# A four-layer graph network on one core: the transpose of layer 2's input moved from TensorE to VectorE and DRAM, layer 0's scaling from VectorE to ScalarE and GpSimd, and a new written order

## The chip, the core and the metric

The kernel runs on one core of a Trainium2 chip. The core has TensorE (PE in the profile, with its weight loads as PEld), VectorE (DVE), ScalarE (ACT), GpSimd (POOL) and SyncE (SP), which here does nothing but issue DMAs; 16 DMA engines move the data. The metric is the time of one execution on the device in microseconds. Before the change the median of three runs is 553.37 us (552.64 to 554.17).

## The reference

32 graphs of 512 nodes with 128 features, all with the same 0/1 adjacency matrix, pass through four layers. Each layer ends with x = layernorm(x + f(x)). In short:

```python
x = _layernorm(x + _L0_gnn_ref(x, adj, ...))   # attention, bias, leaky_relu(0.3)
x = _layernorm(x + _L1_gnn_ref(x, adj, ...))   # attention, elu
x = _layernorm(x + _L2_gnn_ref(x, adj, ...))   # (A*M) @ (x W0) + (A*(1-M)) @ (x W1) + bias
x = _layernorm(x + _L3_gnn_ref(x, adj, ...))   # ((adj @ x + x) W + bias), rows scaled to length 1
```

Layers 0 and 1 form h = x W, two numbers per node, logits leaky_relu(e_src + e_dst, 0.2) masked by the adjacency, a softmax over a row, and the product with h. In layer 2, A is a softmax over the edges of a row (all edges weigh the same for the given inputs) and M the identity, so that a node's own features go through W0 and its neighbours' through W1.

## The kernel before

**Tiles.** A graph is a tile of 128 partitions by 512 columns: four chunks of 128 nodes, side by side. A product with the adjacency over 512 nodes needs 4 x 4 blocks. Where the features have to stand on the partitions, as the stationary side of a product with a weight matrix, x has to be transposed first, for each graph and for layers 0, 1 and 2.

**Units.** The work is written as small named units, each with the tiles it uses (`unit("tb1", "dt1", "xt1")`). For each graph b:

- `ld` and `lb` load x, plainly (L156) and in runs of 32 numbers (L162); `tr0` transposes blocks of 32 x 32 on VectorE (L166), so that `xt0` has layer 0's input transposed.
- `ph0a/b` (L200) form h and its two extra columns, `ex` (L204) their exponentials, `h` (L210) the scaled h. `rt`, `rw`, `rb` (L235, L239, L243) spread a row of exponentials over all partitions by way of DRAM; `al0r` (L255) forms the attention weights on VectorE.
- `po0a/b` (L217) are the attention products, a half of the nodes each; the sum of the weights comes as an extra column and `rs0a/b` (L221) take its reciprocal. `v0a/b` (L262) scale by it and add the bias b0 on VectorE, two instructions per half; `lr` (L272) is the leaky relu, `add0` (L286, GpSimd) the residual, `bn0`, `ms0`, `le0`, `lx0`, `nm0` (L360 to L378) the statistics and `nrm0` (L383, ScalarE) the normalised x1.
- Layer 1 is the same, with x1 transposed by way of DRAM in graphs 3 to 29: `tr1` (L182, VectorE, 32 x 32 blocks), `tw1` (L186, one DMA to DRAM), `tb1` (L192, four DMAs back). In graphs 0, 1, 2, 30 and 31 it goes through TensorE: `pt1` (L174, four transposes into a PSUM bank) and `xt1` (L178, a copy on ScalarE). Its scaling is done on ScalarE (`v1as/v1bs`, L268), and GpSimd normalises x2 (`nrm1p0` to `p3`, L390).
- Layer 2: `xh2` and `xl2` (L292, L296) split x2 into two parts for a fast product, `py2` (L303) multiplies both with the adjacency without its diagonal, `y2` (L307) copies the result. `pt2` and `xt2` (L174, L178) transpose x2 itself, in all 32 graphs. `po2` (L317, L318) adds y2 W1 and xt2 W0 in one PSUM bank; `o2s` (L397) scales by the reciprocal degree, `xb` and `v2p` (L311, L401, GpSimd) add bias and residual.
- Layer 3: `xh3`, `xl3`, `py3`, `y3`, `po3` (L324), `v3` (L328), squares and their root on ScalarE (L334 to L346), `rr0` to `rr3` (L353), `bn3`, `nrm3p0` to `p3` (L390) and the store `st` (L473).

**Order.** Nothing schedules the program but two tables: `STARTS` has a number for each unit that is run once (loads of weights, the transposed adjacency in `an0` to `an3` with its copies `cva` and corrections `cvd`, the final flag that sends unusual inputs to a general path), and `PLAN` one number per unit and graph. The units are sorted by that number and written out, and each engine takes its own in that order. A number of -1 leaves the unit out for that graph. Some 14 graphs are under way at a time. All DMAs of the graphs are issued by SP, in order, each after the semaphores that it needs.

**Buffers.** Each kind of tile has a fixed stock (`kind(...)`): 33 of "sq" for most 128 x 512 tiles, six PSUM banks "ps", four "dt" in DRAM. A tile is taken at its first use in the written order and given back after its last; the engines wait for whatever used it before.

Of the kernel before, what the change touches and what calls it, by code (L numbers as in the profile page):

```python
# [10 lines left out]
F32 = mybir.dt.float32  # L11
# [3 lines left out]
AF = mybir.ActivationFunctionType  # L15
# [3 lines left out]
P = 128  # L19
# [7 lines left out]
def kernel(  # L27
# [87 lines left out]
    def kind(name, count, names, make):  # L115
        STOCK[name] = (count, make)
        for n in names.split():
            KIND[n] = name
# [19 lines left out]
    kind("dt", 4, "dt1", lambda name: dram.tile([P, N], F32, name=name))  # L138
# [4 lines left out]
    def unit(name, *tiles):  # L143
        def register(fn):
            UNITS[name] = (fn, tiles)
        return register
# [33 lines left out]
    @unit("tr1", "x1", "tr1")  # L180
    def _(b, x1, tr):
        nc.vector.transpose(tr.rearrange("p (f c i) -> p c f i", f=NCH, c=NCH), x1)  # L182
# [5 lines left out]
    @unit("tb1", "dt1", "xt1")  # L188
    def _(b, dt, xt):
        for f in range(4):  # L190
            src = bass.AP(tensor=dt.tensor, offset=dt.offset + f * P, ap=[[N, Q], [Q * N, P // Q], [1, P]])
            nc.sync.dma_start(xt[f * Q : (f + 1) * Q, :].rearrange("p (a n) -> p a n", n=P), src)  # L192

# [63 lines left out]
    for half, s in enumerate("ab"):  # L257
# [6 lines left out]

        @unit(f"v1{s}s", f"po1{s}", f"rs1{s}", "o1")
        def _(b, p, rs, o, half=half):
            for c in range(2):
                nc.scalar.activation(chunks(o)[:, 2 * half + c, :], twos(p)[:, c, :F], AF.Copy, scale=rs[:, c : c + 1])  # L268

# [367 lines left out]
    def _(b, p):  # L637
# [3 lines left out]
        "ja": 1, "warm": 2, "awt0": 6, "awc0": 8, "rest": 9, "e2": 10, "awq0": 12, "e0": 13, "am2": 14, "en2": 15,  # L641
        "e1": 16, "aws0": 17, "am0": 18, "e3": 19, "en0": 20, "am1": 24, "eh": 25, "wb": 28, "am3": 29, "m3": 30,
        "m0": 31, "m2": 32, "m1": 33, "en1": 39, "mp": 45, "en3": 46, "an1": 51, "cva1": 54, "dga": 55, "cvd1": 56,
        "deg": 66, "an3": 71, "cva3": 75, "awt1": 80, "cvd3": 81, "awc1": 103, "awq1": 112, "aws1": 116, "an0": 168,
        "cva0": 173, "cvd0": 180, "an2": 270, "cva2": 278, "cvd2": 284, "lpp": 290, "lpd": 357, "de": 525, "dv": 543,
        "out_d": 2946, "out_p": 3099, "out_c": 3104,
    }
    PLAN = {
        "ld": [0, 3, 4, 5, 27, 93, 122, 192, 255, 338, 426, 510, 576, 688, 778, 851, 943, 1020, 1111, 1205, 1308, 1389,
            1469, 1561, 1650, 1741, 1845, 1937, 2020, 2121, 2232, 2281],  # L650
        "pt0": [7, 41, 38, 43, -1, -1, -1, -1, -1, -1, -1, -1, -1, -1, -1, -1, -1, -1, -1, -1, -1, -1, -1, -1, -1, -1,
            -1, -1, -1, -1, -1, -1],
        "xt0": [11, 44, 48, 47, -1, -1, -1, -1, -1, -1, -1, -1, -1, -1, -1, -1, -1, -1, -1, -1, -1, -1, -1, -1, -1, -1,
            -1, -1, -1, -1, -1, -1],
        "ph0a": [21, 57, 76, 77, 125, 132, 166, 264, 331, 420, 496, 608, 640, 747, 831, 941, 1017, 1113, 1200, 1260,
            1416, 1514, 1605, 1701, 1811, 1906, 2017, 2120, 2198, 2312, 2394, 2465],
        "ph0b": [22, 49, 70, 74, 123, 135, 167, 266, 332, 423, 504, 606, 636, 757, 826, 944, 1013, 1118, 1204, 1281,
            1417, 1513, 1603, 1715, 1810, 1908, 2013, 2116, 2200, 2306, 2392, 2528],
        "ex0a": [23, 62, 79, 82, 128, 141, 170, 273, 333, 427, 501, 615, 652, 754, 840, 948, 1024, 1127, 1218, 1280,
            1426, 1523, 1610, 1709, 1820, 1918, 2022, 2127, 2206, 2320, 2404, 2472],  # L660
        "ex0b": [26, 52, 73, 78, 126, 145, 169, 271, 336, 428, 509, 611, 648, 762, 837, 951, 1018, 1123, 1216, 1290,
            1424, 1519, 1609, 1721, 1818, 1915, 2021, 2122, 2205, 2319, 2396, 2536],
        "pc0": [36, 63, 83, 90, 130, 148, 175, 277, 341, 439, 518, 619, 654, 764, 842, 952, 1030, 1130, 1223, 1297,
            1437, 1525, 1617, 1727, 1828, 1923, 2030, 2139, 2208, 2329, 2407, 2538],
        "pr0": [35, 65, 86, -1, -1, -1, -1, -1, -1, -1, -1, -1, -1, -1, -1, -1, -1, -1, -1, -1, -1, -1, -1, -1, -1, -1,
            -1, -1, -1, -1, 2430, 2545],
        "h0a": [42, 68, 87, 95, 131, 156, 184, 289, 345, 447, 530, 635, 658, 767, 859, 957, 1039, 1139, 1236, 1323,
            1441, 1532, 1624, 1736, 1831, 1942, 2038, 2146, 2221, 2338, 2421, 2543],
        "h0b": [37, 64, 84, 91, 133, 150, 177, 283, 342, 441, 519, 621, 655, 765, 844, 953, 1031, 1131, 1225, 1298,
            1438, 1527, 1618, 1728, 1829, 1930, 2031, 2140, 2209, 2330, 2408, 2539],  # L670
        "al0": [40, 72, 96, -1, -1, -1, -1, -1, -1, -1, -1, -1, -1, -1, -1, -1, -1, -1, -1, -1, -1, -1, -1, -1, -1, -1,
            -1, -1, -1, -1, 2434, 2550],
        "po0a": [53, 88, 100, 144, 207, 228, 305, 347, 425, 508, 624, 703, 775, 860, 976, 1022, 1135, 1226, 1309, 1421,
            1517, 1646, 1735, 1815, 1913, 2037, 2137, 2251, 2350, 2435, 2517, 2573],
        "po0b": [60, 98, 114, 159, 215, 253, 320, 364, 453, 554, 646, 716, 795, 908, 960, 1067, 1120, 1263, 1364, 1504,
            1564, 1668, 1767, 1867, 1953, 2066, 2169, 2266, 2366, 2454, 2548, 2641],
        "rs0a": [58, 102, 115, 155, 217, 238, 316, 361, 456, 524, 641, 719, 804, 875, 981, 1048, 1157, 1240, 1329,
            1456, 1534, 1677, 1751, 1869, 1939, 2051, 2172, 2303, 2363, 2450, 2530, 2586],
        "rs0b": [67, 106, 136, 171, 231, 272, 339, 393, 468, 568, 666, 726, 802, 919, 982, 1085, 1165, 1272, 1380,
            1516, 1584, 1685, 1799, 1896, 1964, 2089, 2185, 2294, 2387, 2477, 2565, 2653],  # L680
        "v0a": [59, 107, 117, 178, 232, 248, 322, 362, 465, 529, 643, 728, 811, 885, 987, 1054, 1167, 1248, 1363, 1518,
            1539, 1681, 1777, 1872, 1965, 2059, 2176, 2307, 2370, 2478, 2534, 2591],
        "v0b": [69, 111, 147, 182, 236, 297, 354, 399, 472, 572, 673, 730, 817, 925, 990, 1094, 1178, 1293, 1390, 1544,
            1586, 1688, 1801, 1902, 1970, 2103, 2189, 2322, 2405, 2481, 2572, 2656],
        "lr": [85, 118, 151, 197, 241, 310, 408, 411, 478, 592, 722, 750, 823, 984, 1047, 1146, 1244, 1304, 1448, 1552,
            1596, 1697, 1807, 1917, 1987, 2109, 2212, 2364, 2417, 2486, 2588, 2659],
        "add0": [92, 121, 158, 204, 247, 329, 414, 418, 484, 607, 734, 755, 830, 996, 1057, 1158, 1254, 1319, 1461,
            1563, 1612, 1708, 1813, 1926, 1996, 2119, 2231, 2369, 2422, 2496, 2592, 2663],
# [621 lines left out]
```

## Time and profile before

| | us |
|---|---|
| median of the runs | 553.37 |
| profiled execution | 553.77 |
| its span | 552.1 |
| PE busy | 530.7 |
| DVE busy | 499.1 |
| ACT busy | 472.1 |
| POOL busy | 405.7 |

The granted clock of TensorE over the span is 0.992. The busy time of a group counts each instruction from its start to its end, and instructions of an engine overlap a little; so the cost of a step on a full engine is better read from its start to the next start. Ends of matmuls are modelled. The groups that the change touches, from the page and the answers on lines: the transposes of L174 (164, 148 of them from "sq" tiles, the others from the loaded x), the copies of L178 (41, mean 606 ns), the scale-and-bias of L262 (128, mean 337 ns), the scaling on ScalarE of L268 (128, mean 376 ns), the VectorE transposes of L182 (27, mean 685 ns), and the DMAs of L186 (27 of 256 KB) and L192 (108 of 64 KB). The DMA queue of SP carries 53.94 MB in 123,792 packets, which took 38.4% of the 16 engines' time over the span.

### The profile page before, as it was taken

How to read it: one execution, taken by the hardware profiler on the slowest of the kernel's cores; microseconds unless marked ns; L12 is line 12 of the kernel's file. 1: busy time of each engine (PE TensorE's matmuls, PEld its weight loads, DVE VectorE, ACT ScalarE, POOL GpSimd, SP SyncE). 2: the span in 40 equal slices, each digit the busy share in tenths (PEclk: the TensorE clock that was granted, in tenths of full speed). 3: DMA queues.
4: the chain of work that ended last, by engine and by line, in shares of the span. 5: the costliest groups of instructions: out<-in, count | busy, mean ns of one | idle time of the engine just before them, and what ended most of it. 6: DMA issues, size and time to landing. Idle time of an engine off the chain costs nothing.

```text
span 552.1 us, 13985 instructions
## 1 busy us (share of the span) xinstructions
PE 530.7 (96%) x4116; PEld 501.5 (91%) x4116; DVE 499.1 (90%) x1913; ACT 472.1 (86%) x1868; POOL 405.7 (73%) x673
## 2 busy tenths in 40 slices
PE   7999999999999999999999999999999999999971
PEld 7899999999999999999999999999999999998850
DVE  2799999999999999999999999999999986787475
ACT  3768678988898789888989898898899899989994
POOL 4223795677948868688698776778688878889973
PEclk9999999999999999999999999999999999999996
DMA  7333344536357454446453544545203211000013
GB/s 211 67 83 92 78 117 111 123 93 174 97 136 173 103 139 87 131 112 161 115 136 97 150 106 128 156 99 121 90 20 117 78 39 40 20 21 2 21 57 100
DMA packets 124449, 55.22 MB, mean 100 GB/s; under 512 B 65744, under 2 KB 113488, under 8 KB 124368
## 3 DMA queue, kind: packets, MB, share of 16 engines
q1 hardware_dynamic: 123792, 53.94, 38.4%
q8 instruction: 34, 0.56, 0.4%
q10 hardware_dynamic: 576, 0.33, 0.3%
q14 instruction: 47, 0.39, 0.2%
HBM read 38.67 MB, written 15.58 MB: 98 GB/s over the span
## 4 chain that ended last, share of the span: by engine, by line
PE 76%; DVE 11%; ACT 8%; POOL 2%; issue 1%; DMA 1%; ACTq 0%; DVEq 0%
PE ps L217 37%; PE ps L303 15%; PE ps L200 9%; DVE al L255 4%; PE ps L317 4%; PE ps L318 4%; PE ps L324 4%; PE ps L174 2%; DVE st L360 2%; ACT sq L334 1%; ACT sq L383 1%; DMA acols<-in_L_gnn_a_dst_dram 1%; ACT sq L307 1%; PE ps L230 1%; ACT sq L397 1%
## 5 line engine op out<-in xcount | busy, mean ns | idle before, releaser
L217 PE MATMUL ps<-hp,al 128*128 128x129 f32 x2048 | 244.7, 275 | 0.7 <-POOL off L579 0.5
L217 PEld LDWEIGHTS ps<-hp,al 128*128 128x128 f32 x2048 | 237.4, 191 | 2.7 <-POOL off L579 0.7
L255 DVE SCALAR_TENSOR_TENSOR al<-rb,exps,mp 128x512 f32<-128x512 f32 x216 | 145.6, 735 | 1.2 <-DMA rb<-rd 1.2
L360 DVE BATCH_NORM_STATS2 st<-sq 128x6 f32<-128x128 f32 x508 | 108.2, 274 | 11.1 <-POOL sq L401 7.7
L390 POOL TENSOR_SCALAR sq<-sq,rn 128x128 f32<-128x128 f32 x252 | 113.0, 465 | 3.5
L383 ACT ACTIVATE sq<-sq,rn 128x128 f32<-128x128 f32 x256 | 106.2, 503 | 5.8 <-POOL rn L378 5.6
L210 ACT ACTIVATE hp<-ps,exps 128x128 f32<-128x128 f32 x256 | 89.6, 431 | 0.3
L296 POOL TENSOR_TENSOR xr<-sq,xr 128x512 fp32r<-128x512 f32 x64 | 83.2, 1304 | 7.3 <-DVE st L360 3.8
L200 PE MATMUL ps<-we,sq 128*128 128x131 f32 x512 | 71.2, 277 | 0.1
L303 PE MATMUL ps<-off,xr 128*128 128x512 f32 x256 | 67.6, 406 | 0.0
L303 PE MATMUL ps<-a3t,xr 128*128 128x512 f32 x256 | 67.3, 404 | 0.2 <-POOL xr L296 0.2
L200 PEld LDWEIGHTS ps<-we,sq 128*128 128x128 f32 x512 | 65.4, 192 | 2.0 <-issue 0.5
L286 POOL TENSOR_TENSOR sq<-sq,x 128x512 f32<-128x512 f32 x32 | 41.8, 1307 | 24.0 <-DVE sq L272 13.4
L378 POOL TENSOR_TENSOR rn<-mv,rn 128x4 f32<-128x4 f32 x127 | 28.4, 229 | 41.6 <-ACT rn L374 25.3
L286 POOL TENSOR_TENSOR sq<-sq,sq 128x512 f32<-128x512 f32 x32 | 43.4, 1356 | 17.8 <-DVE sq L280 12.4
L303 PEld LDWEIGHTS ps<-a3t,xr 128*128 128x128 f32 x256 | 46.3, 189 | 10.1 <-POOL xr L296 0.6
L303 PEld LDWEIGHTS ps<-off,xr 128*128 128x128 f32 x256 | 45.9, 189 | 9.1 <-DVE sq L262 0.2
L317 PE MATMUL ps<-w,sq 128*128 128x128 f32 x256 | 49.5, 275 | 0.0
L318 PE MATMUL ps<-w,sq 128*128 128x128 f32 x256 | 49.5, 275 | 0.0
L362 DVE BATCH_NORM_AGGREGATE mv<-st 128x2 f32<-128x9 f32 x508 | 48.7, 157 | 0.0
L401 POOL TENSOR_TENSOR sq<-sq,sq 128x512 f32<-128x512 f32 x32 | 41.1, 1286 | 9.8 <-ACT sq L397 6.9
L268 ACT ACTIVATE sq<-ps,rs 128x128 f32<-128x128 f32 x128 | 39.7, 376 | 8.4 <-DVE rs L221 8.3
(116 smaller groups left out, 918.4 us busy)
## 6 DMA issues: line engine op xcount, KB each, us to landing
rb<-rd SPq DMA_DIRECT2D x54, 256.0 KB, 3.8
x<-in_x_dram SPq DMA_DIRECT2D x32, 256.0 KB, 4.0
out_dram<-sq SPq DMA_DIRECT2D x31, 256.0 KB, 2.3
sw<-in_x_dram SPq DMA_DIRECT2D x112, 64.0 KB, 3.6
dt<-sq SPq DMA_DIRECT2D x27, 256.0 KB, 2.4
sq<-dt SPq DMA_DIRECT2D x108, 64.0 KB, 2.2
rd<-rt SPq DMA_DIRECT2D x54, 2.0 KB, 1.7
an<-in_adj_dram SPq DMA_DIRECT2D x3, 256.0 KB, 4.9
```

The costliest lines, as they stand in the source:

```text
L200: nc.tensor.matmul(twos(p)[:, c, :FE], xt[:, (2 * half + c) * P : (2 * half + c + 1) * P], ATT[k], start=True, stop=True)
L210: nc.scalar.activation(h[:, 2 * half + c, :F], twos(p)[:, c, :F], AF.Identity, bias=pc if k else 0.0, scale=pc)
L217: nc.tensor.matmul(twos(p)[:, c, : F + 1], al[:, j, rows], h[:, j, :], start=(j == 0), stop=(j == NCH - 1))
L255: nc.vector.scalar_tensor_tensor(al[:, j, :], r, exps[:, 2 * b + k, 2, j : j + 1], mask[:, j, :], op0=ALU.max, op1=ALU.mult)
L286: nc.gpsimd.tensor_add(o, o, xk)
L296: nc.gpsimd.tensor_sub(xl, xk, xh.bitcast(F32))
L303: nc.tensor.matmul(p, part[:, j * P : (j + 1) * P], mat[:, j, :], start=(i + j == 0), stop=(i + j == NCH))
L317: nc.tensor.matmul(p[:, cols], y[:, cols], w21, start=True, stop=False)
L318: nc.tensor.matmul(p[:, cols], xt[:, cols], w20, start=False, stop=True)
L360: nc.vector.bn_stats(st[:, c, :6], o[:, c * P : (c + 1) * P])
L383: nc.scalar.activation(xo[:, c * P : (c + 1) * P], o[:, c * P : (c + 1) * P], AF.Identity, bias=rn[:, 1, c : c + 1], scale=rn[:, 0, c : c ...
L390: nc.gpsimd.tensor_scalar(xo[:, c * P : (c + 1) * P], o[:, c * P : (c + 1) * P], rn[:, 0, c : c + 1], rn[:, 1, c : c + 1], op0=ALU.mult, o ...
```

## The change

Three things are changed.

1. In graphs 2 to 30, layer 2's input x2 is transposed as layer 1's is: `tr2` on VectorE in blocks of 32 x 32, `tw2` to DRAM and `tb2` back. The rearrangement is split otherwise than for layer 1: `tw1` writes rows of 2 KB with one DMA and `tb1` reads with four; `tw2` writes with four DMAs, in 512 runs of 128 bytes each, so that `tb2` reads whole rows of 2 KB with one. `pt2` and `xt2` remain in graphs 0, 1 and 31. Layer 1's `tr1`, `tw1`, `tb1` are also used in graphs 2 and 30, where `pt1` and `xt1` go. The stock of DRAM tiles grows from four to six.
2. In graphs 3 to 29, layer 0's scaling by the reciprocal sum is done on ScalarE (`v0as`, `v0bs`: two instructions per half, as `v1as`), and its bias is added after both halves by GpSimd in one instruction over 128 x 512 (`b0p`). In graphs 0, 1, 2, 30 and 31 `v0a/b` remain.
3. Both tables of the order are new.

```diff
-    kind("dt", 4, "dt1", lambda name: dram.tile([P, N], F32, name=name))
+    kind("dt", 6, "dt1 dt2", lambda name: dram.tile([P, N], F32, name=name))
...
-    @unit("tr1", "x1", "tr1")
-    def _(b, x1, tr):
-        nc.vector.transpose(tr.rearrange("p (f c i) -> p c f i", f=NCH, c=NCH), x1)
+    for k in (1, 2):
+
+        @unit(f"tr{k}", f"x{k}", f"tr{k}")
+        def _(b, xk, tr):
+            nc.vector.transpose(tr.rearrange("p (f c i) -> p c f i", f=NCH, c=NCH), xk)
...
+    @unit("tw2", "tr2", "dt2")
+    def _(b, tr, dt):
+        for a in range(NCH):
+            dst = bass.AP(tensor=dt.tensor, offset=dt.offset + a * Q, ap=[[NCH * N, Q], [P, NCH * NCH], [1, Q]])
+            nc.sync.dma_start(dst, tr[a * Q : (a + 1) * Q, :].rearrange("p (g i) -> p g i", i=Q))
+
+    @unit("tb2", "dt2", "xt2")
+    def _(b, dt, xt):
+        nc.sync.dma_start(xt, bass.AP(tensor=dt.tensor, offset=dt.offset, ap=[[N, NCH], [NCH * N, Q], [1, N]]))
...
+        @unit(f"v0{s}s", f"po0{s}", f"rs0{s}", "o0")
+        def _(b, p, rs, o, half=half):
+            for c in range(2):
+                nc.scalar.activation(chunks(o)[:, 2 * half + c, :], twos(p)[:, c, :F], AF.Copy, scale=rs[:, c : c + 1])
...
+    @unit("b0p", "o0")
+    def _(b, o):
+        nc.gpsimd.tensor_tensor(chunks(o), chunks(o), bc(b0_b), op=ALU.add)
```

Of the order, the units run once (the per-graph table changes throughout; the total number of written units goes from 3259 to 3317):

```diff
     STARTS = {
-        "ja": 1, "warm": 2, "awt0": 6, "awc0": 8, "rest": 9, "e2": 10, "awq0": 12, "e0": 13, "am2": 14, "en2": 15,
...
-        "deg": 66, "an3": 71, "cva3": 75, "awt1": 80, "cvd3": 81, "awc1": 103, "awq1": 112, "aws1": 116, "an0": 168,
-        "cva0": 173, "cvd0": 180, "an2": 270, "cva2": 278, "cvd2": 284, "lpp": 290, "lpd": 357, "de": 525, "dv": 543,
-        "out_d": 2946, "out_p": 3099, "out_c": 3104,
...
+        "en0": 29, "mp": 30, "m0": 32, "m3": 33, "en1": 37, "en3": 43, "awt1": 54, "an2": 56, "awc1": 58, "an3": 59,
+        "dga": 60, "awq1": 61, "an0": 62, "aws1": 63, "an1": 64, "cva3": 67, "deg": 68, "cva0": 70, "cvd3": 73,
+        "cva1": 74, "cvd0": 75, "cva2": 78, "cvd1": 80, "cvd2": 86, "lpp": 266, "lpd": 316, "dv": 434, "de": 1002,
+        "out_d": 3020, "out_p": 3156, "out_c": 3177,
     }
```

The numbers count places in the written order, not microseconds.

## The prediction

> **What bounds the kernel now.** I read the page's busy times first, then the chain that ended last, the busy times by stretch, the single instructions in order of time for the cost of a step, and the DMA issues and SP's waits. The page, busy time and the chain's shares by engine:
>
> ```profile
> PE 530.7 (96%) x4116; PEld 501.5 (91%) x4116; DVE 499.1 (90%) x1913; ACT 472.1 (86%) x1868; POOL 405.7 (73%) x673
> ...
> PE 76%; DVE 11%; ACT 8%; POOL 2%; issue 1%; DMA 1%; ACTq 0%; DVEq 0%
> ```
>
> Busy time by stretch (from:to, length, then PE, PE's weight loads, DVE, ACT, POOL with counts; granted clock, DMA share, GB/s):
>
> ```profile
> 175.00:225.00 50.00, 50.00 (x416) 48.53 (x414) 49.82 (x192) 42.77 (x165) 37.10 (x59) 1.00 0.52 123
> 325.00:375.00 50.00, 50.00 (x398) 47.82 (x397) 49.81 (x182) 44.08 (x176) 38.59 (x64) 1.00 0.51 131
> 500.00:520.00 20.00, 19.90 (x135) 17.95 (x134) 13.08 (x71) 19.47 (x82) 20.00 (x27) 1.00 0.05 15
> 540.00:552.10 12.10, 0.48 (x2) 0.29 (x2) 6.33 (x32) 5.99 (x33) 3.29 (x9) 0.63 0.30 92
> ```
>
> In the middle PE is full at full clock and DVE nearly so; ACT has 12 to 14% free, POOL 23 to 26%. The chain in order of time is made of PE pieces alone from 125 to 480 us, and of mixed pieces after:
>
> ```profile
> 473.17 3.57 PE ps L217 x32
> 478.52 1.87 PE ps L303 x8
> 480.87 2.73 DVE al L255 x4
> ```
>
> So PE sets the pace. From start to next start, a half of the attention product (16 matmuls) takes 1.785 us, a half of h 0.447, the two aggregations 1.95 each, po2 1.78, po3 0.89, four transposes 0.44. One graph: 4 x 1.785 + 4 x 0.447 + 2 x 1.95 + 1.78 + 0.89 + 0.44 = 15.9 us; all steps sum to 527. I laid the start of each PE step in the trace beside the sum of the PE work written before it: PE is 6 us late at its first ph0, 10 late at 33 us of work, and stays 8 to 11 late up to py3 of graph 29. It loses time only at both ends: 10 us at the start, about 4 before the last py3 (starts at 535.4), and 16.7 from there to the end.
>
> **The change, part by part.** Step costs from instructions in order of time (start, duration, engine, line):
>
> ```profile
> 259.90 0.60 PE L174 MATMUL ps<-ident,sq 128*128 128x128 f32 x4
> 260.34 1.84 PE L217 MATMUL ps<-hp,al 128*128 128x129 f32 x15
> 260.95 0.65 ACT L178 COPY sq<-ps 128x512 f32<-128x512 f32 x1
> 261.43 0.70 ACT L268 ACTIVATE sq<-ps,rs 128x128 f32<-128x128 f32 x2
> ...
> 207.44 0.60 DVE L262 SCALAR_TENSOR_TENSOR sq<-ps,rs,b_b 128x128 f32<-128x128 f32 x2
> 207.96 0.86 DVE L360 BATCH_NORM_STATS2 st<-sq 128x6 f32<-128x128 f32 x4
> ...
> 200.71 0.70 DVE L182 STREAM_TRANSPOSE sq<-sq 128x512 f32<-128x512 f32 x1
> 201.33 2.67 DVE L255 SCALAR_TENSOR_TENSOR al<-rb,exps,mp 128x512 f32<-128x512 f32 x4
> ...
> 212.04 1.12 ACT L268 ACTIVATE sq<-ps,rs 128x128 f32<-128x128 f32 x4
> 213.12 0.18 ACT L204 ACTIVATE exps<-ps 128x6 f32<-128x6 f32 x1
> ```
>
> Start to next start: a set of four PE transposes 0.44 us, its copy on ACT 0.48, a scale-and-bias pair on DVE 0.52, a DVE transpose 0.62, four scalings on ACT 1.08.
>
> PE: pt2 goes in 29 graphs and pt1 in 2 more (graphs 2 and 30): 31 x 0.44 = -13.6 us. Each set also held one of the six PSUM banks; I count no gain for that, as PE doesn't wait for a bank in the middle.
>
> DVE: 27 graphs lose two pairs, 27 x 1.04 = -28.1; 31 transposes come, 31 x 0.62 = +19.2; net -8.9. Per graph PE drops by 0.44 and DVE by 0.42: should the 99% on DVE be the bound and not PE, the gain is nearly the same.
>
> ACT: +27 x 1.08 = +29.2, less 31 copies, -14.9; net +14.3, or 0.6 per graph. From 44.1 of 50 us it does 14.0 us per 15.9; it would do 14.6 per 15.5. I cost it at nothing because PE's work covers it; with the cover gone it costs up to 0.6 per graph, 16 us.
>
> POOL: b0p is a 128x512 two-input add, as L311 (1.28 us each on the page): +27 x 1.28 = +34.6; 12.3 per graph becomes 13.6. Hidden as well; the cover is 1.9 us per graph. The Trainium skill speaks against it ("SBUF — State Buffer", Who interferes with whom): a DVE instruction with two SBUF inputs and a GpSimd instruction that reads SBUF exclude each other for a whole instruction. Such DVE steps are lr (L272, mean 721 ns) and elu (L280, 771), beside 681 for L328, one input of which is in PSUM: 0.04 to 0.09 us each with POOL at 77%. By the row, POOL at 88% adds about 1 us in all; by the rule, each b0p holding up one DVE step for its 1.28 us, 35. I take the row.
>
> The waits that come with it: b0p waits on POOL for v0bs, with norm pieces and residual adds of other graphs behind it; lr then waits on DVE for b0p, with the al of other graphs behind it, for which PE's product waits. The new order leaves a median of 4 us of PE work between b0p and lr, at least 1.8.
>
> SP and DMA: per graph four tw2 issues like the 128-byte loads of sw and one tb2 like dt, and in two graphs a tw1 and four tb1. Tiles by name, duration min/median/max in ns; the page's DMA issues with us to landing; SP's waits:
>
> ```profile
> L162 SPq DMA_DIRECT2D sw<-in_x_dram x112: 422/488/2226, 13.2 to 383.1; - x112
> ...
> sw<-in_x_dram SPq DMA_DIRECT2D x112, 64.0 KB, 3.6
> dt<-sq SPq DMA_DIRECT2D x27, 256.0 KB, 2.4
> ...
> SPq L243 <- DMA rd<-rt: 33.0, 25, 3.0
> SPq L192 <- DMA dt<-sq: 11.7, 11, 2.6
> ```
>
> 4 x 0.49 + 0.35 = 2.3 us of SP per graph. By the medians of their lines SP issues per graph ld 0.44, sw 4 x 0.49, rd 2 x 0.48, rb 2 x 0.36, dt 0.35, tb1 4 x 0.43 and the store 0.40, 6.5 us now, and waits for landings (33.0 + 11.7) / 27 = 1.7; it would be 10.5 of 15.5 plus the new wait of tb2 for tw2. Behind tb2 on SP stand rb (DVE's al waits for it) and tb1 (PE's ph1 waits for it).
>
> DMA engines: the trace's packets of 128 bytes took a mean 14 ns (58,208 of them), those of 512 bytes 28, of 2 KB 111. tw2 is 2048 of the first, tb2 128 of the last: (28.7 + 14.2) / 16 = 2.7 us per graph on a share of 0.51, so 0.69. Here a rule of the Trainium skill weighs more: "DMA: Bandwidth & Descriptors", Specifications, wants 512 bytes for line rate and says that below this an engine reads, modifies and writes. The only short writes to DRAM in this trace are rd's; the 96 such packets after 390 us, where no sw load runs, took 12 ns each, less than the reads. By the row tw2 is 1.8 us of all engines; by the rule, a 512-byte read and a write for each run, 2 x 28 = 56 ns, 7.2 us, and the share 1.0 (8.1 + 7.2 + 0.9 = 16.2 us per 15.5). I take the row, since it is a write of this very kind.
>
> Order: the early steps an0 to an3 with their copies and corrections, of which two sets came at places 168 to 284 in the old order, now all lie within the first graphs: 0.9 us on PE, 2 on ACT, 1.8 on POOL, at a time when ACT is busy 18.5 of 25 us (25 to 50): 0 to 1 us, I take 0.
>
> The end: when the old order reaches po1a of graph 31 (485.6 us, 477.2 of PE work done), 49.8 us of PE and 53.1 of ACT work are left, 45.6 and 46.1 of it before the last py3, which took 49.8: ACT's work plus 3.7. The new order has 474.4 of PE work before that step, 39.1 of PE and 43.3 of ACT left, 34.9 and 37.3 of it before py3: its last graphs lie further forward. So po1a at 474.4 + 8.4 = 482.8, py3 at 482.8 + 37.3 + 3.7 = 523.8, and the end 16.7 later: **span 540.5**, 11.6 less than 552.1. Of the 13.6 taken from PE about 2 are lost because ACT, with more to do, sets the end. The profiled execution is 553.77 for a span of 552.10, the runs' median 0.4 below it: 540.5 + 1.67 - 0.4 = 541.8, **542 us**.
>
> **Rivals.** First, *SP held by tw2* (slower). One queue issues in order, and tb2 must see tw2 landed. SP has 15.5 - 10.5 = 5.0 us per graph for that wait; with more than 5.4 the kernel is slower than now (15.9 per graph). A landing takes 2.4 (dt) to 3.6 us (sw), and the new order puts 4.5 us or more of PE work between tw2 and tb2, 6.3 in the median, filled with other issues; against it, sw issues of up to 2.2 us show that bursts of short runs hold SP, and the new order has four tw2 and a sw load within 10 us of PE work. At a 6 us wait: 16.5 per graph, 29 x 0.6 = +17, 570 us. The rule's price for a write would lead here too.
>
> Second, *PE waits for xt1*: tb1 to ph1 has a median of 5.0 us of PE work between (8.4 before), at least 3.6, and a tb1 takes 1.3 to its last issue and 2.2 to land. With landings 1 to 2 us later nearly each graph would show it. PE's loss is the greatest lateness, not the sum, while SP keeps its rate: 5 to 9 us, so 547 to 551. Third, *nothing gained*: ACT or the chain through b0p takes the pace and 13 us come back as waits: 553.
>
> **How the numbers follow.** Forecast 0.70 (537 to 547), second rival 0.10, third 0.06, first 0.14. About 0.3% (1.7 us) can be told from no change. Faster 0.80, same 0.06, slower 0.14. The low end, 537, is all 13.6 and 3 us less of drain; the range reaches to 553 to take in the second and third rival and leave out 0.2.
>
> **What would show it.** Right: L174 down to about 40 transposes, PE's sum down by 14 and still 50 of 50 in the middle, ACT at 47 and POOL at 43 to 44 of 50, DMA share near 0.7, SP's wait for the landing of tw2 below 60 us in all. Wrong: idle time of PE ahead of L200 or L217 ended by xt or al, a DMA share at 0.9 or more, rb or tb1 landing 2 us later than now, or sw and tw2 issues held for microseconds.

## The result and the profile after

The changed kernel takes **600.92 us** in the median (597.98 to 602.2) beside 553.0 for the kernel before: a ratio of 1.086 (95% interval 1.081 to 1.090). The forecast was 542, faster. The profiled execution took 600.56 us for a span of 598.9. New line numbers of the units that matter: `tr1`/`tr2` L184, `tw1` L188, `tb1` L194, `tw2` L200, `tb2` L204, `ph` L212, `po` L229, `rw` L251, `rb` L255, `al` L267, `v0as`/`v0bs` L280, `b0p` L289, `lr` L293, `po2` L338 and L339.

The page after, busy times and the chain's shares by engine and by line:

```profile
PE 538.0 (90%) x3992; PEld 503.0 (84%) x3992; DVE 495.6 (83%) x1836; ACT 484.5 (81%) x1945; POOL 442.5 (74%) x700
...
PE 34%; DVE 22%; DMA 20%; ACT 11%; SPq 6%; POOL 4%; issue 3%; DVEq 0%; ACTq 0%; POOLq 0%
PE ps L229 17%; DMA sq<-dt 9%; DVE al L267 9%; PE ps L324 6%; PE ps L212 5%; DMA rb<-rd 4%; DVE st L381 4%; DMA rd<-rt 4%; ACT sq L404 2%; PE ps L339 2%; PE ps L338 2%; PE ps L345 2%; DVE sq L184 2%; SPq L200 2%; ACT hp L222 1%
```

The counts are as the change says: 124 matmuls fewer on PE (31 x 4), 27 more additions on POOL. But no engine is full any more. The chain, 76% PE and 1% DMA before, is now 34% PE and 20% DMA, with 6% in SP's issues.

Busy time by stretch of the kernel after (columns as before):

```profile
175.00:225.00 50.00, 41.08 (x301) 38.10 (x299) 40.84 (x150) 39.15 (x150) 35.23 (x56) 0.97 0.57 134
325.00:375.00 50.00, 46.02 (x344) 43.51 (x344) 38.86 (x143) 43.61 (x178) 39.28 (x63) 0.97 0.58 137
575.00:599.00 24.00, 9.19 (x40) 6.67 (x40) 14.98 (x77) 14.91 (x82) 12.24 (x28) 0.67 0.27 80
```

From 175 to 225 us PE does 301 matmuls where it did 416 before, and the share of the DMA engines is 0.57, less than the 0.69 forecast: the engines as a whole are not full. All of the loss is in the middle. The last `py3` of the kernel starts at 581.8 and the end comes 17.1 us later; before, it was 535.4 and 16.7.

What was waited for on the compute engines (us in total, times, longest), after:

```profile
DVE al L267 <- DMA rb<-rd: 21.8, 12, 5.5
POOL sq L422 <- ACT sq L418: 21.3, 7, 6.6
PEld ps L339 <- DMA sq<-dt: 17.0, 6, 6.0
...
PE ps L339 <- DMA sq<-dt: 15.8, 6, 5.8
PE ps L212 <- DMA sq<-dt: 15.0, 5, 4.8
```

PE waits for xt2 (L339) and for xt1 (L212), and DVE for rb: 21.8 us in all now, where the kernel before had

```profile
DVE al L255 <- DMA rb<-rd: 1.2, 1, 1.2
```

Three different transfers are late, two of which the change doesn't touch. Beside it SP's own waits and its issues by tile (min/median/max ns):

```profile
SPq L255 <- DMA rd<-rt: 31.0, 19, 3.9
...
SPq L204 <- DMA dt<-sq: 7.3, 10, 1.5
```

```profile
L200 SPq DMA_DIRECT2D dt<-sq x116: 548/627/3311, 91.2 to 547.4; - x116
...
L204 SPq DMA_DIRECT2D sq<-dt x29: 542/567/2956, 97.2 to 549.7; - x29
```

The first rival, tb2 waiting on SP for the landing of tw2, is not what happened: 7.3 us in ten waits. But single issues took up to 3.5 us. One place shows it, SP's instructions in order of time (start, duration):

```profile
152.08 0.57 SPq L204 DMA_DIRECT2D sq<-dt  x1
152.69 5.09 SPq L162 DMA_DIRECT2D sw<-in_x_dram  x4
157.88 2.13 SPq L255 DMA_DIRECT2D rb<-rd  x1
```

After the tb2 at 152.08 four loads of sw take 5.09 us to issue instead of some 2, and the rb behind them 2.13 instead of 0.4. SP isn't waiting for a semaphore there; it is held in the issue itself.

**Landings.** The page's list of DMA issues gives no landing time for the kernel after. In the table each issue of SP is put beside its packets in the trace, in order and by packet size. Median us from issue to last packet, after the first 100 us:

| | ld | sw | rd | rb | tw1 | tb1 | tw2 | tb2 |
|---|---|---|---|---|---|---|---|---|
| before | 3.25 | 2.45 | 1.29 | 3.31 | 2.06 | 1.73 | | |
| after | 3.98 | 2.28 | 1.97 | 3.54 | 2.70 | 1.92 | 1.94 | **5.37** |

Where transfers with packets of one size overlap, this pairing can give a packet to the wrong one. The updates of the semaphore that each DMA raises when it lands don't have that fault, and the landing times of the other pages are taken from them. By them tb2 lands in 6.14 us, dt in 3.23 (2.55 before) and rd in 3.00 (1.70 before).

tb2 moves 256 KB in packets of 2 KB, as `dt` does (tw1, a write, 2.06 in the table before the change) and rb (a read like tb2, 3.31). It needs 2.6 and 1.6 times as long. Its access pattern in DRAM is `[[N, 4], [4N, 32], [1, N]]`: the slowest dimension is 4, where tw1's is 128. That became the first theory: **tb2 runs on four DMA engines**. The Trainium skill has the rule in "DMA: Bandwidth & Descriptors", under "Why a DMA increments its semaphore by 16 and not by 1" (How many engines): a DMA is spread over the largest k up to 16 that divides the slowest dimension of both its sides. For 4 and 128 that is 4. The trace gives no engine number for a packet, but it agrees in two counts. Every DMA of the kernel before and of `n_k16` (below) raises its semaphore in 16 updates; each tb2 of the kernel after does it in five, one soon after the issue (0.98 us in the median) and four at the landing. And SP's queue carries 9348 packets of 4 bytes in the kernel after and 9712 in `n_k16`: 12 fewer for each of the 29 tb2, and 16 for one load that `n_k16` adds. What four engines cost has to be shown by time.

### The profile page after: what moved, and what is told of

Read it like the earlier page. It is cut to its first block, busy times and chain, and to the rows that moved or that the text cites. A ratio compares the mean times of both kernels' runs of the same rounds, so it can differ in the third digit from the quotient of the medians.

```text
span 598.9 us, 14031 instructions
## 1 busy us (share of the span) xinstructions
PE 538.0 (90%) x3992; PEld 503.0 (84%) x3992; DVE 495.6 (83%) x1836; ACT 484.5 (81%) x1945; POOL 442.5 (74%) x700
## 4 chain that ended last, share of the span: by engine, by line
PE 34%; DVE 22%; DMA 20%; ACT 11%; SPq 6%; POOL 4%; issue 3%; DVEq 0%; ACTq 0%; POOLq 0%
PE ps L229 17%; DMA sq<-dt 9%; DVE al L267 9%; PE ps L324 6%; PE ps L212 5%; DMA rb<-rd 4%; DVE st L381 4%; DMA rd<-rt 4%; ACT sq L404 2%; PE ps L339 2%; PE ps L338 2%; PE ps L345 2%; DVE sq L184 2%; SPq L200 2%; ACT hp L222 1%
## 5 line engine op out<-in xcount | busy, mean ns | idle before, releaser
L229 PE MATMUL ps<-hp,al 128*128 128x129 f32 x2048 | 252.6, 279 | 5.1 <-DVE al L267 4.6
L229 PEld LDWEIGHTS ps<-hp,al 128*128 128x128 f32 x2048 | 244.6, 195 | 10.8 <-DVE al L267 4.8
L267 DVE SCALAR_TENSOR_TENSOR al<-rb,exps,mp 128x512 f32<-128x512 f32 x216 | 145.8, 736 | 22.0 <-DMA rb<-rd 21.8
L222 ACT ACTIVATE hp<-ps,exps 128x128 f32<-128x128 f32 x256 | 88.2, 435 | 0.1
L212 PE MATMUL ps<-we,sq 128*128 128x131 f32 x512 | 72.0, 285 | 16.0 <-DMA sq<-dt 15.0
L212 PEld LDWEIGHTS ps<-we,sq 128*128 128x128 f32 x512 | 65.9, 197 | 19.0 <-issue 14.2
L324 PE MATMUL ps<-a3t,xr 128*128 128x512 f32 x256 | 68.8, 412 | 0.0
L339 PE MATMUL ps<-w,sq 128*128 128x128 f32 x256 | 53.2, 291 | 15.8 <-DMA sq<-dt 15.8
L307 POOL TENSOR_TENSOR sq<-sq,x 128x512 f32<-128x512 f32 x32 | 44.8, 1400 | 20.6 <-DVE sq L293 16.5
L422 POOL TENSOR_TENSOR sq<-sq,sq 128x512 f32<-128x512 f32 x32 | 40.9, 1277 | 25.0 <-ACT sq L418 21.3
L339 PEld LDWEIGHTS ps<-w,sq 128*128 128x128 f32 x256 | 41.5, 204 | 17.1 <-DMA sq<-dt 17.0
L338 PE MATMUL ps<-w,sq 128*128 128x128 f32 x256 | 51.9, 286 | 1.3 <-ACT sq L328 1.3
L285 ACT ACTIVATE sq<-ps,rs 128x128 f32<-128x128 f32 x128 | 39.9, 376 | 13.5 <-DVE rs L233 13.0
L418 ACT ACTIVATE sq<-ps,rdeg 128x128 f32<-128x128 f32 x128 | 36.8, 384 | 16.6 <-PE ps L339 16.4
```

The lines of the kernel that those rows point to most:

```text
L212: nc.tensor.matmul(twos(p)[:, c, :FE], xt[:, (2 * half + c) * P : (2 * half + c + 1) * P], ATT[k], start=True, stop=True)
L222: nc.scalar.activation(h[:, 2 * half + c, :F], twos(p)[:, c, :F], AF.Identity, bias=pc if k else 0.0, scale=pc)
L229: nc.tensor.matmul(twos(p)[:, c, : F + 1], al[:, j, rows], h[:, j, :], start=(j == 0), stop=(j == NCH - 1))
L267: nc.vector.scalar_tensor_tensor(al[:, j, :], r, exps[:, 2 * b + k, 2, j : j + 1], mask[:, j, :], op0=ALU.max, op1=ALU.mult)
L307: nc.gpsimd.tensor_add(o, o, xk)
L324: nc.tensor.matmul(p, part[:, j * P : (j + 1) * P], mat[:, j, :], start=(i + j == 0), stop=(i + j == NCH))
```

## The experiments

The theories: (A) tb2's four engines, (B) the layer-2 path with its extra issues and short runs, wherever it runs, (C) the layer-0 part, (D) the new order itself is too tight. All times are medians, beside 552.3 to 553.9 for the kernel before on the same chip.

### The parts alone, in the old order

`o_l0`: the old order with only the layer-0 part, its units added as in the change.

```diff
+ for s in "ab":
+     PLAN[f"v0{s}s"] = [-1] * B
+     for b in range(3, 30):
+         PLAN[f"v0{s}s"][b], PLAN[f"v0{s}"][b] = PLAN[f"v0{s}"][b], -1
+ PLAN["b0p"] = [max(PLAN["v0as"][b], PLAN["v0bs"][b]) + 0.5 if 3 <= b < 30 else -1 for b in range(B)]
```

> The old order with layer 0's part alone: scaling on ScalarE at the places of the VectorE steps, b0p right after the later half; layer 2 as before. PE's work is as before. Theory 'four engines' (and short runs): no cost of its own, 551 to 556 us. Rival 'chain through b0p': above 562.

Measured 587.97, ratio 1.063 (1.058 to 1.069). The waits of this kernel:

```profile
POOL sq L289 <- ACT sq L280: 24.9, 20, 2.3
...
DVE sq L293 <- POOL sq L289: 19.7, 13, 3.1
...
DVE st L381 <- POOL sq L307: 13.9, 16, 2.4
```

The chain ACT, POOL, DVE for one tile has three engines in it where one had been, and an order that leaves no work between them makes each wait for the one before. So the part costs 35 us where the order isn't made for it. Here the theory 'four engines' missed, and the rival's "above 562" came true; whether the part also costs that in its own order is for `n_nodma` below to say.

`o_l2`: the old order with only the layer-2 part, in graphs 2 to 28.

```diff
+ for n in ("tr2", "tw2", "tb2"):
+     PLAN[n] = [-1] * B
+ for b in range(2, 29):
+     t, u = PLAN["pt2"][b], PLAN["po2"][b]
+     PLAN["tr2"][b], PLAN["tw2"][b], PLAN["tb2"][b] = t, t + 0.2, t + 0.35 * (u - t) + 0.3
+     PLAN["pt2"][b] = PLAN["xt2"][b] = -1
```

> The old order with layer 2's part alone, graphs 2 to 28: tr2 at pt2's place, tw2 right after, tb2 a third of the way to po2 (several us before it is needed), tb2 as changed, on its slowest dimension of 4. Layer 0 as before. PE's work falls by 12 us. Theory 'four engines': po2 has room, but four engines are crowded and rb and tb1 land later: 548 to 575 us, with waits of al on rb and ph1 on xt1. Rival 'order': the old order has wider margins and the new one is the cause: 540 to 546. Rival 'short runs and SP': 565 or more.

Measured 616.51, ratio 1.115 (1.109 to 1.121): above the 548 to 575 of the four engines, on the side of the rival 'short runs and SP'.

`n_dve_v0`: the new order and the layer-2 part, but layer 0 scaled on VectorE as before, without `b0p`.

```diff
+ for s in "ab":
+     for b, t in enumerate(PLAN[f"v0{s}s"]):
+         if t >= 0:
+             PLAN[f"v0{s}"][b], PLAN[f"v0{s}s"][b] = t, -1
+ PLAN["b0p"] = [-1] * B
```

> The changed kernel in its own order, with layer 0 scaled and biased on VectorE in all graphs again, at the places of the ScalarE steps; b0p is left out. Theory 'four engines': the DMA waits stay, 590 to 605 us. Rival 'chain through b0p': POOL's step and the waits behind it are the cause, below 575.

Measured 608.24 in a single run, DVE busy 517.1 instead of 495.6. The changed kernel's runs lie between 598.0 and 602.2, so in the new order the layer-0 part seems to gain some 7 us; the order was not made for the kernel without it. (C) is not the cause of the 48 us, and what `o_l0` showed is the price of a part without its order; `n_nodma` says the same with repeated runs.

### Sixteen engines for tb2

`n_k16`: the changed kernel with the rows read back in the order in which they lie in DRAM. They then stand on other partitions, so W0's rows are loaded a second time in the same order; the product is the same.

```diff
- nc.sync.dma_start(xt, bass.AP(tensor=dt.tensor, offset=dt.offset, ap=[[N, NCH], [NCH * N, Q], [1, N]]))
+ nc.sync.dma_start(xt, dt)
...
- nc.tensor.matmul(p[:, cols], xt[:, cols], w20, start=False, stop=True)
+ nc.tensor.matmul(p[:, cols], xt[:, cols], w20p if PLAN["tb2"][b] >= 0 else w20, start=False, stop=True)
...
```

> The changed kernel in its own order; only tb2's read is laid out so that its slowest dimension is the 128 partitions and not four chunks of rows (xt2's features stand in another order, and W0 has its rows in that order for these graphs, one more 64 KB load). Theory 'four engines': tb2's one DMA of 128 rows runs on 4 of the 16 DMA engines, because its slowest dimension is 4; it lands after 5.4 us where rb, of the same 128 packets of 2 KB, lands after 3.5, PE waits for xt2 in po2, and what other DMAs have on those four engines waits behind it. Then: tb2 lands within 3.7 us, the waits of po2 on xt2 (16 us) nearly vanish, tw1 and tb1 land 0.3 us or more earlier, 545 to 565 us. Rival 'short runs and SP': the 2048 runs of 128 bytes per graph and SP's issue time (tw2 0.67 us each where I counted 0.49) are the cause: 585 to 600.

Measured **559.39**, ratio 1.012 (1.007 to 1.018): one access pattern gives back 41 of the 48 us. tb2 lands in 2.64 instead of 5.37 (2.99 instead of 6.14 by the semaphores), and the page gives landing times again. The busy times of its page, and the waits that answer to those above:

```profile
PE 520.2 (93%) x3992; PEld 488.2 (88%) x3992; DVE 494.6 (89%) x1836; ACT 481.4 (86%) x1945; POOL 443.4 (80%) x700
```

```profile
DVE al L267 <- DMA rb<-rd: 10.7, 12, 2.3
...
PE ps L212 <- DMA sq<-dt: 7.4, 4, 2.2
...
PEld ps L339 <- DMA sq<-dt: 3.8, 2, 2.6
```

All three have shrunk, those for rb and xt1 too. PE's busy time for the same 3992 matmuls falls from 538.0 to 520.2; this is taken up in the last section.

`n_four`: tb2 in its own layout, as four DMAs of 32 rows.

```diff
- nc.sync.dma_start(xt, bass.AP(tensor=dt.tensor, offset=dt.offset, ap=[[N, NCH], [NCH * N, Q], [1, N]]))
+ for c in range(NCH):
+     src = bass.AP(tensor=dt.tensor, offset=dt.offset + c * N, ap=[[NCH * N, Q], [1, N]])
+     nc.sync.dma_start(xt[c * Q : (c + 1) * Q, :], src)
```

> The changed kernel with its own layout in DRAM; tb2 is four DMAs of 32 rows each instead of one of 128 (slowest dimension 32): it can use all 16 engines, and SP issues three DMAs more per graph. Theory 'four engines': near n_k16, 558 to 572 us. Rival 'the number of DMAs that SP issues' or 'W0's other row order in n_k16 made the difference': 595 or more.

Measured 574.74, ratio 1.040 (1.037 to 1.042): 26 us better than one DMA of slowest dimension 4, 15 worse than one of 128, and 3 above the top of what was expected. The bytes, the packets and W0 are those of the changed kernel; the pattern and the number of DMAs differ. Each of the four raises its semaphore in 16 updates again. Three further issues per graph cost 5 us in `n_long4` below; where the other 10 come from is open.

`o_l2_k16`: `o_l2` with tb2 over sixteen engines, as in `n_k16`.

> o_l2 (old order, layer 2's part alone in graphs 2 to 28) with tb2 over all engines as in n_k16. Theory 'four engines': 25 to 50 us less than o_l2's 616.5, 566 to 592 us, the rest from VectorE, which gets 17 us more work in an order that left it 1% idle, and from rb behind tw2 on SP. Rival 'order alone': still above 600.

Measured 600.16, ratio 1.087 (1.083 to 1.090): 16 us better than `o_l2`, outside the range and by a hair on the side of the rival 'order alone'. So in the old order four engines cost 16 us, and the rest of the layer-2 part 48 (600.2 beside 552.4). VectorE has the transposes on top there (514.0 us of work instead of 499.1) and waits 25.6 us for rb. Whether the part lacks the layer-0 part or the new order was not tested apart.

### What the sum would have been: the path taken away, piece by piece

`n_nodma`: tw2 and tb2 are left out in all graphs, and po2's second product reads a constant tile, so that layer 2's own term is not computed from x2.

```diff
- @unit("po2", "y2", "xt2", "po2")
- def _(b, y, xt, p):
+ @unit("po2", "y2", "po2")
+ def _(b, y, p):
+     xt = ej[:, 0, :]
...
+ for b in range(B):
+     PLAN["tw2"][b] = PLAN["tb2"][b] = -1
```

> The changed kernel in its own order with tw2 and tb2 left out in all graphs; tr2 stays on VectorE, and po2's second product reads a constant tile in place of xt2, so layer 2 lacks the nodes' own features (all matmuls are there). Theory 'four engines, and the rest is waiting for late DMAs': with that path gone PE has no waits in the middle, and my sum without allowance for waits holds: 539 to 545 us. Rival 'the order and layer 0's part cost it by themselves': 553 or more.

Measured **544.49**, ratio 0.986 (0.982 to 0.989); its span is 541.7. The new order and the layer-0 part, then, cost nothing by themselves. Its page and two stretches of its middle:

```profile
PE 517.0 (95%) x3992; PEld 488.0 (90%) x3992; DVE 493.3 (91%) x1836; ACT 481.0 (89%) x1945; POOL 444.0 (82%) x700
```

```profile
175.00:225.00 50.00, 50.00 (x397) 47.80 (x396) 48.67 (x179) 47.51 (x198) 42.49 (x66) 1.00 0.51 124
325.00:375.00 50.00, 50.00 (x389) 47.44 (x388) 47.21 (x173) 47.98 (x196) 45.14 (x67) 1.00 0.57 138
```

`n_long`: `n_k16`, with tw2 as one DMA of 128 rows of 2 KB. The regrouping into runs of 128 bytes is left out, so xt2 holds x2 in another arrangement.

```diff
- for a in range(NCH):
-     dst = bass.AP(tensor=dt.tensor, offset=dt.offset + a * Q, ap=[[NCH * N, Q], [P, NCH * NCH], [1, Q]])
-     nc.sync.dma_start(dst, tr[a * Q : (a + 1) * Q, :].rearrange("p (g i) -> p g i", i=Q))
+ nc.sync.dma_start(dt, tr)
```

> n_k16 (tb2 over all engines) with tw2 as one DMA of 128 rows of 2 KB instead of four with 2048 runs of 128 bytes: the bytes are the same, the regrouping is left out, so layer 2's own term reads a wrong layout. Theory 'short runs and SP's issues cost the rest' (16 to 17 us of waits left in n_k16): 541 to 549 us. Rival 'DMA latency in a tight order costs the rest, whatever the runs': 553 to 560.

Measured 545.48, ratio 0.988 (0.985 to 0.990). Its middle, by stretch, looks as the forecast said it would: PE 50 of 50, ACT at 47 to 48, share near 0.7:

```profile
325.00:375.00 50.00, 50.00 (x389) 47.44 (x389) 47.16 (x173) 47.70 (x197) 46.01 (x68) 1.00 0.68 170
```

`n_long4`: the same with four DMAs of 32 rows each; the regrouping is left out here too.

```diff
- nc.sync.dma_start(dt, tr)
+ for a in range(NCH):
+     nc.sync.dma_start(dt[a * Q : (a + 1) * Q, :], tr[a * Q : (a + 1) * Q, :])
```

> New order, the read of dt2 over 16 engines, and tw2 as four DMAs of 32 whole rows of 2 KB: the regrouping into 128-byte runs is left out, so layer 2's first product reads rows in another arrangement. Between the kernel with four short-run DMAs (559.4) and the one with one long-row DMA (545.5) lie 14 us. If the number of issues on SP costs them: 555 to 560, with SP's time per tw2 issue near 0.5 us or more. If the length of the runs does: 545 to 549, with about 0.35 us per issue.

Measured 550.45, ratio 0.996 (0.994 to 0.997), between the two expectations: both count. Three further issues per graph cost 5 us, the short runs 9 more (to 559.4). The issues of tw2 on SP, first in `n_long4`, then in `n_k16`:

```profile
L199 SPq DMA_DIRECT2D dt<-sq x116: 302/422/1949, 89.4 to 498.5; - x116
```

```profile
L200 SPq DMA_DIRECT2D dt<-sq x116: 548/627/1990, 89.6 to 508.7; - x116
```

An issue of 32 rows takes 0.42 us, one of 512 runs of 128 bytes 0.63. From `n_nodma` up the medians make a ladder: 544.5 without the path, 545.5 with long rows, 550.5 with three issues more, 559.4 with short runs, 600.9 with tb2 on four engines.

`n_rshort`: `n_k16` with the short runs on the side of the read. tw2 is one DMA of whole rows, tb2 four DMAs that read runs of 128 bytes; nothing of the work is left out.

```diff
- nc.sync.dma_start(xt, dt)
+ for a in range(NCH):
+     src = bass.AP(tensor=dt.tensor, offset=dt.offset + a * Q * N, ap=[[P, P], [Q, NCH], [1, Q]])
+     nc.sync.dma_start(swapped2(xt)[:, :, a], src)
...
```

> New order, tw2 as one DMA of whole rows, and the regrouping moved to the read: tb2 is four DMAs that read runs of 128 bytes. The same result, the same bytes and the same number of short packets as the kernel with 16 engines, now on the read side. If short runs and four issues cost the same on either side: 555 to 565 (later rather than earlier, as the four stand behind the wait for the landing). If only short writes are slow: 545 to 550.

Measured 561.92, ratio 1.016 (1.013 to 1.020): the price is nearly the same on either side. An issue takes 0.63 us here too:

```profile
L207 SPq DMA_DIRECT2D sq<-dt x116: 523/628/1906, 96.9 to 517.8; - x116
```

A price that only short writes have doesn't show.

`n_k16_tb1`: `n_k16`, with layer 1's tb1 as one DMA instead of four (a second copy of the attention matrix with its rows in the same order).

```diff
- for f in range(4):
-     src = bass.AP(tensor=dt.tensor, offset=dt.offset + f * P, ap=[[N, Q], [Q * N, P // Q], [1, P]])
-     nc.sync.dma_start(xt[f * Q : (f + 1) * Q, :].rearrange("p (a n) -> p a n", n=P), src)
+ src = bass.AP(tensor=dt.tensor, offset=dt.offset, ap=[[P, P], [Q * N, NCH], [1, P]])
+ nc.sync.dma_start(xt.rearrange("p (a n) -> p a n", n=P), src)
```

> The kernel with 16 engines, and layer 1's tb1, which was four DMAs, made one over 16 engines, with the attention matrix of layer 1 in the matching row order in a second tile. SP loses three issues of 0.43 us and more per graph, and xt1 is there earlier. If the 14 us left come from SP's queue and from late xt1: 546 to 553, with PE's wait for xt1 gone to under 3 us. If they come from the 128-byte packets alone: 556 to 560.

Measured 556.91, ratio 1.010 (1.006 to 1.013): 2.5 us below `n_k16`, which is within the spread of the runs (554.8 to 560.1 beside 558.2 to 562.6). It lies in the 556 to 560 of the 128-byte packets, and not in the 546 to 553 of SP's queue. PE's wait for xt1 is 4.0 us, in one wait. It has the lowest median of the variants that leave no work out, and is not faster than the kernel before.

### Who pays for four engines

`n_nowait`: the changed kernel with every DMA as it is, tb2 on four engines included; only po2's second product reads a constant tile, so that layer 2's own term is left out and nobody reads xt2.

```diff
  @unit("po2", "y2", "xt2", "po2")
  def _(b, y, xt, p):
+     if PLAN["tb2"][b] >= 0:
+         xt = ej[:, 0, :]
```

> The changed kernel with all its DMAs, tw2 and tb2 on four engines included, but po2's second product reads a constant tile in place of xt2 (its result is left out of the product): nobody waits for tb2's landing. If the 41 us that four engines cost come from TensorE's own waits for xt2 and the half clock after them: 548 to 563, since 25.5 us of such waits and most of 14 us go. If four loaded DMA engines hold up the other transfers, which then hold up ph1 and al: 575 to 595.

Measured **595.88**, ratio 1.077 (1.074 to 1.080). Of the 41 us only some 5 go: 0.9 above the range of the second theory, and far from the first. PE's own waits for xt2 stood out after the change and are nearly irrelevant. They come back elsewhere; the waits of this kernel:

```profile
DVE al L267 <- DMA rb<-rd: 28.6, 14, 5.5
...
PE ps L212 <- DMA sq<-dt: 23.0, 4, 11.1
```

PE now waits for xt1, once for 11.1 us. So what costs is what tb2 does to the transfers behind it. Put beside each other, transfers that SP issued within 5 us after a tb2 and all others, median us from issue to last packet (45 to 500 us):

| | ld | sw | rd | rb | sw, mean us of issue |
|---|---|---|---|---|---|
| after, within 5 us of tb2 | 5.11 | 3.31 | 3.09 | 4.47 | 0.93 |
| after, others | 3.58 | 2.09 | 1.61 | 3.38 | 0.56 |
| n_k16, within 5 us of tb2 | 3.06 | 2.59 | 1.98 | 3.28 | 0.64 |
| n_k16, others | 2.98 | 2.22 | 1.66 | 3.40 | 0.56 |

Behind a four-engine tb2 each of these kinds lands 1.1 to 1.5 us later; behind a sixteen-engine one at most 0.4. By the semaphores the difference is larger, as some packets are paired with the wrong DMA here: sw 5.6 us against 3.2, rd 4.9 against 2.4, tb1 5.0 against 2.5, rb 5.2 against 4.0 in the kernel after. In `n_k16` it is at most 0.7 for the same four.

The semaphores also show where the time goes. The rd that is issued at 150.88, 0.7 us behind a tb2, has 12 of its 16 updates by 152.55 and the other four from 155.26 to 156.63; that tb2's own four come from 155.04 to 156.42. Of the 68 DMAs issued within 3 us after a tb2 (45 to 500 us), 49 have a pause of more than 0.5 us between their 12th and 13th update; in `n_k16` none of 79 has. So twelve engines go on, and four make most of what is issued behind a tb2 wait.

Issues longer than 2 us, 45 to 500 us: 10 in the kernel after, 10 in `n_nowait`, 1 in `n_k16`, 2 before. Nine of the ten in the kernel after end within 0.35 us of the last update of a tb2 that was issued before them: SP gets on when tb2's four engines are done.

`b_four` and `b_sixteen`: is this the price of the transfer, or of the new order? The kernel before, whole, with one more read per graph into a tile that nobody reads, at the place of xt2 in the old order.

```diff
+ extra = const.tile([P, 448], F32, name="extra")
...
+ @unit("xx")
+ def _(b):
+     nc.sync.dma_start(extra, bass.AP(tensor=x.tensor, offset=x[b].offset, ap=[[N, NCH], [NCH * N, Q], [1, 448]]))
...
+ PLAN["xx"] = [PLAN["xt2"][b] + 0.5 if 2 <= b <= 30 else -1 for b in range(B)]
```

`b_sixteen` has `ap=[[N, P], [1, 448]]` instead.

> The kernel before, unchanged in its work and its order, with one more read per graph in graphs 2 to 30: 128 rows of 1792 bytes of the input into a tile that nobody reads, put where the copy of layer 2's transpose stands in the order, with the access pattern of tb2 (slowest dimension 4). If the four-engine transfer itself is the price, through the transfers behind it on SP's queue: slower by 10 us or more (563 to 600), with rb and sw landing later and SP's issues held. If it costs only in an order without slack such as the new one: 552 to 557.

> The same with the plain access pattern (slowest dimension 128), so that the read is spread over 16 engines. Both theories: 552 to 556, as TensorE sets the pace and SP has some 5 us free per graph. Above 560 here would say that any further transfer costs, and not the four engines.

Measured: `b_four` **566.82**, ratio 1.024 (1.020 to 1.029); `b_sixteen` **553.39**, ratio 1.0006 (0.9986 to 1.0026). The same bytes cost 14 us or nothing, so the transfer itself is the price. The extra read's issues on SP (min/median/max ns), first `b_four`, then `b_sixteen`:

```profile
L197 SPq DMA_DIRECT2D extra<-in_x_dram x29: 529/602/1317, 81.0 to 509.0; - x29
```

```profile
L197 SPq DMA_DIRECT2D extra<-in_x_dram x29: 328/457/1132, 81.7 to 490.8; - x29
```

And DVE's wait for rb, which has nothing to do with that read, in the same two kernels:

```profile
DVE al L260 <- DMA rb<-rd: 11.5, 5, 4.8
```

```profile
DVE al L260 <- DMA rb<-rd: 2.7, 3, 1.6
```

Of the DMAs issued within 3 us after the extra read, 47 of 64 have the pause after their 12th update in `b_four`, and none of 66 in `b_sixteen`.

No other transfer of these kernels has packets of 1792 bytes, so they can be told apart in the trace. One took a mean of 93 ns in `b_four` and 97 in `b_sixteen`; from the first to the last of the 128 it was 3.67 us against 1.31, and from issue to the last 5.10 against 2.69. Packets of 93 ns, 32 after another, are 3.0 us: four engines fit, sixteen (0.8) don't. That settles (A) without the change's order. The price depends on where the transfer stands: 14 us here and 16 in `o_l2` against `o_l2_k16`, both in the old order, and 41 in the new. As `n_nodma` and `n_long` show, the new order costs nothing where no transfer is late (D).

## Why the prediction was wrong

The forecast was 542 and faster; the kernel takes 600.9, 48 us slower than before. The steps, in the prediction's own words:

**"tw2 is 2048 of the first, tb2 128 of the last: (28.7 + 14.2) / 16 = 2.7 us per graph"**: this failed. It assumes that a transfer is spread over 16 engines. For tb2 the division is 14.2 / 4 = 3.6 us on each of four engines, four times its term. As a mean over 16 the share was right (0.69 forecast; 0.67 to 0.71 in `n_k16`, 0.68 in `n_long`), which is why the share raised no alarm: a mean share can't show that four of sixteen are crowded. `n_k16` prices the step at 41 us.

**"A landing takes 2.4 (dt) to 3.6 us (sw)"**: failed for tb2. dt's row was the nearest by bytes and packet size; the access pattern, which stands in the diff, differs. By the same measure tb2 lands in 6.14, and in 2.99 over sixteen engines.

**"with landings 1 to 2 us later nearly each graph would show it. PE's loss is the greatest lateness, not the sum, while SP keeps its rate: 5 to 9 us"**: the second rival had the right symptom (landings later by 1 us and more behind each tb2) and the wrong arithmetic, since SP didn't keep its rate: its issues were held for up to 3.5 us. PE's stops add up. Set beside the written order, PE lost 54.7 us between 45 and 500 us in the changed kernel and 16.9 in `n_k16`; its single idle times are 5.8 and 2.4 us at most.

**First rival, "SP held by tw2"**: its side of the outcome was right and its mechanism wrong. tb2's waits for tw2 are 7.3 us in all, longest 1.5, far from the 5.4 per graph at which it decides; the sign "SP's wait for the landing of tw2 below 60 us in all", named for a right forecast, came true in a kernel 48 us slower. SP was held by tb2, not by the wait for tw2. The section on what would show the forecast wrong did name the signs: "sw and tw2 issues held for microseconds", PE stopped by xt.

**"4 x 0.49 + 0.35 = 2.3 us of SP per graph"**: mis-sized. tw2 issues take 0.67 in the mean, tb2 0.66: 3.3. Taking the price of an sw load was right in kind (512 runs of 128 bytes), but its median of 0.49 hid a mean of 0.63 after the first 100 us.

**The sum of 540.5 holds no allowance for waits in the middle.** With sixteen engines PE's stops there are 16.9 us; 540.5 + 16.9 = 557.4, close to `n_k16`'s span of 557.1. `n_long4` and `n_long` say what most of it is: 5 us for three further issues per graph, 9 for the short runs. Both were costed at nothing, because SP had 5 us per graph to spare; but slack in the mean is not slack at the place where the transfer is due.

What held:
- PE -13.6: 530.7 to 517.0 in `n_nodma`, where PE hardly waits in the middle. POOL +34.6: 405.7 to 444.0 there, +38. ACT +14.3: +9 there, +12 in the changed kernel. DVE -8.9: -4 to -6, in part since `lr` (L293) went from 721 to 811 ns in `n_nodma`, 2.9 us in all. The exclusion of the Trainium skill ("SBUF — State Buffer", Who interferes with whom) does show there: where POOL is busy for over 70% of an lr (17 of them) it takes 917 ns in the mean, where for under 30% (13) 671. But the price that the prediction worked out from it, 35 us, was rightly not taken: the row's 1 us was off by 2, the 35 by 32.
- The end: py3 of the last graph was forecast at 523.8 and the end 16.7 later; in `n_nodma` it is 525.2 and 16.5. Forecast span 540.5, span of `n_nodma` 541.7. So every part of the change but the path through DRAM was worth what the sum said: 544.5, 8 us faster.
- "I take the row" for the write of short runs: the price worked out from the read-modify-write of the Trainium skill ("DMA: Bandwidth & Descriptors", Specifications), 56 ns per run and a share of 1.0, is not there. The share is 0.7, the 128-byte packets of `n_k16` after 405 us, all but 64 of 18,496 of them tw2's, took a mean of 12.7 ns, and reads were as dear as writes (`n_rshort`). But the row missed that short runs cost on SP and in landing rather than on the DMA engines.

Two things are not settled. What holds SP in an issue until tb2's four engines are done is argued: a transfer on SP's one queue seems not to be accepted while its share has no room on a crowded engine; no record shows the queues' fill. And whether all 29 tb2 use the same four engines is shown only where two come close together: two tb2 issued 0.9 us apart (548.86 and 549.74) end 2.9 us apart, as one after the other on the same engines would; in `n_k16` the same two end 0.8 apart. With four engines for all, their load, of the 15.5 us per graph, would be (8.1 + 1.8) + 3.6 = 13.5 us, an estimate of 0.87 against 0.64 for the rest.

## What to carry to other kernels

Before the bytes of a DMA are divided by 16, read the slowest dimension of its access pattern on both sides: with 4 there, 256 KB here took 5.4 us to the last packet instead of 2.6 and held up what was issued behind it, which cost 14 to 16 us in the old order and 41 in the tight new one, while the mean share of the DMA engines looked harmless. When a wait appears in the profile, ask what it would cost if nobody waited for it: taking PE's visible wait for xt2 away gave back 5 of 41 us, since the damage was done to the transfers behind it on the same queue. A change in three parts with an order of its own can't be judged by its parts in the old order: the layer-0 part costs 35 us there and, by a single run, gains 7 in its own.

## What the runs showed of the hardware

**The pattern, not the bytes.** `b_four` against `b_sixteen`: equal packets (93 and 97 ns), 3.67 against 1.31 us from first to last, 566.8 against 553.4 us for the kernel.

**Stops of PE cost twice.** In the kernel after, the granted clock drops to one half for spells of 3.4 us, or twice that, at or after stops of PE. The stretches of two of them:

```profile
153.30:160.10 6.80, 3.63 (x17) 3.63 (x18) 2.74 (x5) 2.37 (x13) 3.48 (x5) 0.50 0.54 133
207.90:211.30 3.40, 2.80 (x13) 2.80 (x14) 2.90 (x19) 0.54 (x3) 0.00 (x0) 0.50 0.55 123
```

There are eight such spells between 45 and 500 us in the kernel after, 30.7 us in all, one in `n_k16` and none before. PE is busy for 53 to 100% of each, 25.9 us in all; at half speed about half of that, an estimated 13 us, is lost. "TensorE: Matmul & The Clock Gate" in the Trainium skill (Part 1: The HAM clock gate) gives the same window of 3.4 us, and an idle window as the cause. Here less was enough: seven of the eight follow a single stop of PE of 2.0 to 5.8 us, four of them shorter than 3.4, in a kernel in which PE is busy for 90%. The first sets in 0.2 us after its stop begins, which stays open. The half clock is most of why PE is busy for 538.0 us with the work that takes it 520.2 in `n_k16`.

**Runs of 128 bytes are dear to issue.** 0.63 us for 512 runs against 0.42 for 32 rows of 2 KB, the same 64 KB, whether the runs are on the side of the write or of the read.
